# Dividing attention by its sums in packed feature lanes: four PE transposes a token block replaced by DMAs through DRAM

## The chip, the cores and the metric

The kernel runs on one core of a Trainium2 chip, as one launch. The metric is the device time of that launch in microseconds. Engines are named as the profile names them: PE (matrix), DVE (vector), ACT (scalar), POOL, and SP, whose queue issues most of the DMAs. The tile framework puts the waits between engines; within an engine instructions run in the order in which they stand, and a DMA's wait holds up everything behind it in its queue.

## What is computed

Two transformer layers over x of shape (8, 512, 256), float32, 16 heads of 16 features, a layer norm after each residual. Layer 0 is a masked softmax attention and a mixture of experts with a capacity of 512 tokens an expert. Layer 1 normalises q and k inputs by their mean square, rotates q and k, and takes sigmoid weights in place of exponentials; its mixture has eight experts and four that pass x through. What matters here:

```python
# layer 0: keys j at or behind query i
scores = einsum('bhid,bhjd->bhij', q, k) * 0.25
attn = softmax(where(j >= i, scores, -inf), -1)
out = einsum('bhij,bhjd->bhid', attn, v)
# layer 1
weights = sigmoid(einsum('bhqd,bhkd->bhqk', q, k) * 0.25)
weights = weights / (sum(weights, -1, keepdims=True) + 1e-8)
attn = einsum('bhqk,bhkd->bhqd', weights, v)
# both
x = layernorm(x + attn.reshape(8, 512, 256) @ o_w.T + o_b)
```

Both divide only after the weighted sum over v: the values carry a seventeenth column of ones for each head, so that the sum of the weights comes out beside the head's 16 features.

## The kernel before, in words

**Waves.** Each sequence's attention runs in 16 waves. A wave makes one block of scores for four heads (`scores`, L583 and L1021), ACT takes the exponential or sigmoid, and the wave after adds the weights times v into a PSUM bank (`gathered`, L607 and L1039). The four heads' lanes lie 32 apart: 16 features, one sum, 15 empty ones. After every fourth wave the bank is copied by ACT into `o`, a tile of 128 lanes by (t, m, token); t and m pick the head within its lane group. So o of sequence a is whole shortly after the next sequence b = a + 1 has begun its waves.

**From o to the projection.** In the waves of b, steps for a are placed by hand. `by_token` (L623, L1055; four a sequence) turns 128 tokens of o with four PE transposes into a bank of PSUM, where DVE takes the reciprocal of the 16 sums of a token and multiplies, into `ao` (token by feature). `by_feature` (L642, L1075; two a sequence) turns ao back with four transposes and a copy into `aoT` (feature by token). `projected` (L653, L1089) multiplies aoT by wo_s, four matmul groups a sequence, and adds the residual. The banks that these steps use (`bank`, tag mm) are one in layer 0 and two in layer 1.

**Order.** Within `tc.manual_schedule` the order on each engine is that of the program. `beside0(b, w)` and `beside1(b, w)` hold the plan of wave w: lists that run after the wave's scores (`first`), after the gather (`second`), and in layer 1 a third behind both. In layer 0 each wave also makes `greatest`, the search of row maxima six waves ahead, whose four reductions are DVE's largest work. Layer 1's plan also holds `query`, a part of q or k: after the second part ACT adds the bias (`raw`), POOL and DVE rotate it (L1009 to L1012), and for k DVE makes `kb` (L1017). `value`, `turned_in`, `normed` and `residual` prepare sequence n = b + 1.

**Other stages.** The steps of sequence 6 of layer 0 are laid into the gaps of that layer's expert matmuls (the list at L1624), those of sequence 7 into layer 1's first waves (L1540), and those of sequence 7 of layer 1 into the first blocks of its experts (L1831), each block of which is loaded by `load` (L1687), on SP, two blocks ahead.

**SP's queue** loads x, the weights and the blocks, and blanks DRAM buffers of layer 1 (`fill`, L472: per sequence 16 transfers of 272 KB and two of 512 KB, in four parts at waves 0, 4, 8 and 12). Layer 1's weights are issued where `layer1` is called, between waves 31 and 32 of layer 0 (L1607), and first read by PE in the first step of `router_steps` (`turn`, L277), in sequence 2's first wave. None of these waits for computed data until L1406 loads the tokens of the experts, so SP's place in the program says little of when it issues.

Of the kernel before, what the change touches and what calls it, by code (L numbers as in the profile page):

```python
# [9 lines left out]
FP = mybir.dt.float32  # L10
# [3 lines left out]
ALU = mybir.AluOpType  # L14
# [3 lines left out]
P = 128  # L18
# [5 lines left out]
NHS = 4  # L24
# [19 lines left out]
def tile_two_layers(  # L44
# [174 lines left out]
    def project(ps, w, hs, xT):  # L219
        for kc in range(KC):  # L220
            nc.tensor.matmul(
                out=ps, lhsT=w[:, kc, hs * P : (hs + 1) * P], rhs=xT[:, kc, :],
                start=(kc == 0), stop=(kc == KC - 1),
            )
# [136 lines left out]
    def layer0():  # L361
# [261 lines left out]
        def by_token(b, c):  # L623
            q = st[b]
            ps = bank()
            for t in range(2):
                for m in range(2):
                    nc.tensor.transpose(
                        ps[:, (2 * t + m) * P : (2 * t + m + 1) * P],
                        q["o"][:, t, m, c * P : (c + 1) * P], ident,  # L630
                    )
            ps = ps.rearrange("p (t h x) -> p t h x", t=2, x=32)
            rec = small.tile([P, 2, 8], FP, tag="rec", name="rec")
            nc.vector.reciprocal(rec, ps[:, :, :, HD])
            if c == 0:
                q["ao"] = att.tile([P, NC, D], FP, tag="ao", name=f"ao{b}")
            nc.vector.tensor_tensor(
                q["ao"][:, c, :].rearrange("p (h t x) -> p t h x", t=2, x=HD),
                ps[:, :, :, :HD], rec.unsqueeze(3).to_broadcast([P, 2, 8, HD]), ALU.mult,
            )  # L640

        def by_feature(b, kc):  # L642
            q = st[b]
            if kc == 0:
                q["aoT"] = att.tile([P, KC, S], FP, tag="aoT", name=f"aoT{b}")
            ps = bank()
            for c in range(NC):
                nc.tensor.transpose(
                    ps[:, c * P : (c + 1) * P], q["ao"][:, c, kc * P : (kc + 1) * P], ident
                )  # L650
            nc.scalar.copy(q["aoT"][:, kc, :], ps)
# [197 lines left out]
    def layer1(turns):  # L849
# [205 lines left out]
        def by_token(b, c):  # L1055
            q = st[b]
            ps = bank()
            for t in range(2):
                for m in range(2):
                    nc.tensor.transpose(  # L1060
                        ps[:, (2 * t + m) * P : (2 * t + m + 1) * P],
                        q["o"][:, t, m, c * P : (c + 1) * P], ident,
                    )
            ps = ps.rearrange("p (t h x) -> p t h x", t=2, x=32)
            rec = small.tile([P, 2, 8], FP, tag="rec", name="rec")
            nc.vector.tensor_scalar(rec, ps[:, :, :, HD], TINY, None, ALU.add)
            nc.vector.reciprocal(rec, rec)
            if c == 0:
                q["ao"] = att.tile([P, NC, D], FP, tag="ao", name=f"ao{b}")
            nc.vector.tensor_tensor(  # L1070
                q["ao"][:, c, :].rearrange("p (h t x) -> p t h x", t=2, x=HD),
                ps[:, :, :, :HD], rec.unsqueeze(3).to_broadcast([P, 2, 8, HD]), ALU.mult,
            )

        def by_feature(b, kc):  # L1075
            q = st[b]
            if kc == 0:
                q["aoT"] = att.tile([P, KC, S], FP, tag="aoT", name=f"aoT{b}")
            ps = bank()
            for c in range(NC):  # L1080
                nc.tensor.transpose(
                    ps[:, c * P : (c + 1) * P], q["ao"][:, c, kc * P : (kc + 1) * P], ident
                )
            if kc == 0:
                nc.vector.tensor_copy(q["aoT"][:, kc, :], ps)
            else:
                nc.scalar.copy(q["aoT"][:, kc, :], ps)
# [202 lines left out]
    def beside0(b, w):  # L1290
# [13 lines left out]
            1: ([(t.by_token, a, 0)], [(t.turned_in, n, 1), (t.pointed, z)]),  # L1304
            2: ([], [(t.query, n, 0, "q", 0), (t.residual, n), (t.kept, z, 0)]),
            3: ([(t.query, n, 0, "q", 1)], [(t.query, n, 0, "k", 0), (t.kept, z, 1)]),
            4: ([(t.by_token, a, 1)], [(t.by_token, a, 2), (t.counted, z)]),
            5: ([(t.by_token, a, 3)], [(t.ranked, z)]),
            6: ([], [(t.query, n, 0, "k", 1), (t.sent, z), (t.kept, z, 2)]),
            7: ([(t.by_feature, a, 0)], [(t.by_feature, a, 1), (t.kept, z, 3)]),  # L1310
# [44 lines left out]

    AHEAD = 6
    waiting = None

    def waves0(start, stop):
        nonlocal waiting  # L1360
        t = l0
        for g in range(start, stop):
            b, w = g // 16, g % 16
            now = None
            if g >= 0:
                now = t.scores(b, w // 8, w // 4 % 2, NC - 1 - w % 4)
                if w % 4 == 0:
                    t.fill(b, w // 4)
                if w == 10 and b + 2 < B:
                    t.load_x(b + 2)  # L1370
# [147 lines left out]
    def beside1(b, w):  # L1518
# [4 lines left out]
            0: ([], [(t.query, b, 1, "q", 1)], []),  # L1523
            1: ([(t.by_token, a, 0)], [(t.by_token, a, 1)], [(t.summed, n, 0), (t.scatter, z, 0)]),
            2: ([(t.by_token, a, 2)], [(t.by_token, a, 3)], [(t.summed, n, 1), (t.scatter, z, 1)]),
            3: ([], [(t.query, b, 1, "k", 0)], [(t.summed, n, 2), (t.scatter, z, 2)]),
            4: ([], [(t.query, b, 1, "k", 1)], []),
            5: ([(t.by_feature, a, 0)], [(t.by_feature, a, 1)], [(t.summed, n, 3), (t.scatter, z, 3)]),
            6: ([(t.projected, a, 0)], [], [(t.normed, n), (t.gather, f, 0)]),
            7: ([(t.projected, a, 1)], [(t.turned_in, n, 0)], [(t.residual, n), (t.gather, f, 1)]),  # L1530
            8: ([(t.projected, a, 2)], [(t.turned_in, n, 1)], [(t.gather, f, 2)]),
            9: ([(t.projected, a, 3)], [(t.query, n, 0, "q", 0)], [(t.normed3, a), (t.gather, f, 3)]),
            10: ([], [(t.query, n, 0, "q", 1)], [(t.logits, a)]),
            11: ([], [(t.query, n, 0, "k", 0)], [(t.chosen, a)]),
            12: ([], [(t.query, n, 0, "k", 1)], []),
            13: ([(t.value, n, 0)], [(t.value, n, 1)], [(t.counted, a)]),
            14: ([(t.value, n, 2)], [(t.ranked, a)], [(t.sent, a)]),
            15: ([(t.value, n, 3)], [(t.query, n, 1, "q", 0)], []),
        }
        if b == 0:  # L1540

            u, a = l0, B - 1
            for i, (first, second, third) in {
                0: ([(t.value, 0, 2)], [(t.query, 0, 1, "q", 0)], []),
                1: ([(t.value, 0, 3), (u.by_token, a, 0)], [(u.by_token, a, 1)], []),
                2: ([(u.by_token, a, 2)], [(u.by_token, a, 3)], []),
                5: ([(u.by_feature, a, 0)], [(u.by_feature, a, 1)], []),
# [52 lines left out]
    with tc.manual_schedule():  # L1600
# [20 lines left out]
        waiting = None  # L1621
        a, z, n = B - 2, B - 3, B - 1
        t = l0
        steps = [(t.by_token, a, 0), (t.query, n, 1, "q", 0), (t.by_token, a, 1), (t.query, n, 1, "q", 1)]  # L1624
        steps += [(t.by_token, a, 2), (t.query, n, 1, "k", 0), (t.by_token, a, 3), (t.query, n, 1, "k", 1)]
        steps += [(t.by_feature, a, kc) for kc in range(KC)]
        steps += [(t.kept, z, c) for c in range(NC)]
# [441 lines left out]
```

## Time and profile before

| | us |
|---|---|
| three runs, median (lowest to highest) | 1525.03 (1523.87 to 1526.2) |
| the profiled execution | 1510.96 |
| its span, first to last instruction | 1509.2 |

The mean granted PE clock of the profiled execution was 0.973. By stage, from the busy times of windows:

| stage | us | PE | DVE | ACT | POOL | DMA share |
|---|---|---|---|---|---|---|
| start and sequence 0 of layer 0 | 0 to 104 | 89.4 | 53.0 | 46.8 | 25.8 | 0.76 |
| layer 0's attention, sequences 1 to 6 | 104 to 520 | 390.6 | 283.2 | 215.4 | 134.2 | 0.32 |
| layer 0's experts | 520 to 735 | 212.3 | 48.1 | 34.2 | 0.0 | 0.24 |
| layer 0's last sequence, layer 1's first waves | 735 to 830 | 84.6 | 55.7 | 44.8 | 40.6 | 0.10 |
| layer 1's attention | 830 to 1273 | 429.2 | 311.7 | 288.2 | 180.7 | 0.16 |
| layer 1's expert blocks and the end | 1273 to 1509 | 201.1 | 127.8 | 61.8 | 99.0 | 0.64 |

A row of a group reads: line, engine, operation, tile written <- tiles read, shapes, count | busy us in all, mean ns of one | idle us of its engine just before, with the release that ended most of it. A row of a timeline reads: start, duration, engine, line, operation, count merged into the row [idle before <- what ended it]. One f32 matmul leaves two records, so a group of four matmuls is x8. A row of DMA issues gives the count, KB of each and the median us from issue to landing; SPq is SP's queue.

### The profile page before, as it was taken

What the parts mean: (1) busy time and instruction counts of PE and PEld (TensorE: products, weight loads), DVE (VectorE), ACT (ScalarE), POOL (GpSimd) and SP (SyncE); (2) the same over time, 40 slices, a digit from 0 to 9 for tenths busy, and PEclk for the clock granted to TensorE, in tenths of its full rate; (3) what the DMA queues carried; (4) which work ended last, traced back from release to release, by engine and by line L of the source; (5) the groups of instructions that cost most, each with busy time, mean ns of one, the idle gap of its engine ahead of it and who ended that gap; (6) DMA issues with size and microseconds to landing.
All of it is one profiled execution on the core that took longest, in us unless ns stands there. A gap on an engine that the chain in (4) does not pass through costs nothing. (4 is left out here: it accounts for less than half of the span.)

```text
span 1509.2 us, 24812 instructions
## 1 busy us (share of the span) xinstructions
PE 1407.2 (93%) x8574; PEld 762.1 (51%) x8574; DVE 879.6 (58%) x3287; ACT 691.2 (46%) x1079; POOL 480.3 (32%) x602
## 2 busy tenths in 40 slices
PE   7999989999998899999989999999999999999991
PEld 4444444444444466776534333334333334888881
DVE  4556666776767512321365766876876855553494
ACT  3455545555555321111235656666666665222242
POOL 2322233333233200000252224544653440442462
PEclk9999999999999999999979999999999999999996
DMA  9959960000000013223010000202302005677864
GB/s 243 265 149 355 358 229 17 14 13 19 7 23 4 30 49 119 84 84 98 29 42 6 24 9 30 41 27 24 46 26 25 20 20 168 185 219 214 281 218 157
DMA packets 136011, 149.86 MB, mean 99 GB/s; under 512 B 29646, under 2 KB 118891, under 8 KB 135875
## 3 DMA queue, kind: packets, MB, share of 16 engines
q1 hardware_dynamic: 118274, 121.51, 25.6%
q0 software_dynamic: 10560, 23.51, 6.1%
q10 hardware_dynamic: 7040, 3.15, 0.8%
q8 instruction: 72, 1.18, 0.3%
q14 instruction: 65, 0.52, 0.1%
HBM read 76.88 MB, written 77.10 MB: 102 GB/s over the span
## 5 line engine op out<-in xcount | busy, mean ns | idle before, releaser
L569 DVE CUSTOM_DVE_ANT_0 seen<-sc,shade 128x128 f32<-128x128 f32 (+3 forms) x512 | 250.9, 490 | 131.8 <-PE sc L561 102.4
L1035 ACT ACTIVATE e<-sc 128x1024 f32<-128x1024 f32 x256 | 248.3, 1021 | 148.9 <-PE sc L1027 147.4
L600 POOL TENSOR_SCALAR_AFFINE_SELECT e<-e 128x256 f32<-128x256 f32 x256 | 104.8, 414 | 576.9 <-ACT e L597 574.0
L597 ACT ACTIVATE e<-sc 128x1024 f32<-128x1024 f32 (+3 forms) x256 | 168.2, 702 | 129.8 <-PE sc L588 120.5
L588 PE MATMUL sc<-q,k 32*128 32x512 f32 (+3 forms) x1024 | 140.6, 500 | 7.6 <-DVE mpad L569 7.0
L1044 PE MATMUL av<-e,v 128*32 128x512 f32 x1024 | 139.6, 612 | 0.0
L561 PE MATMUL sc<-k,q 32*128 32x384 f32 (+3 forms) x1024 | 120.8, 489 | 5.8 <-DVE mpad L569 4.6
L612 PE MATMUL av<-e,v 128*32 128x512 f32 (+3 forms) x1024 | 101.2, 464 | 2.7 <-POOL e L600 2.3
L1457 PE MATMUL sc<-wo,h 128*128 128x256 f32 x448 | 99.2, 380 | 0.0
L1748 PE MATMUL yp<-w_e,h 128*128 128x256 f32 x416 | 96.2, 384 | 2.2 <-DVE h L1740 2.2
L1440 PE MATMUL sc<-xeT,wi 128*128 128x512 f32 x224 | 98.3, 592 | 0.0
L1732 PE MATMUL sc<-xtT,w_e 128*128 128x256 f32 x416 | 94.2, 379 | 0.0
L588 PEld LDWEIGHTS sc<-q,k 32*128 32x128 f32 x1024 | 57.9, 190 | 66.7 <-issue 36.7
L1457 PEld LDWEIGHTS sc<-wo,h 128*128 128x128 f32 x448 | 84.3, 190 | 11.5 <-issue 0.5
L1748 PEld LDWEIGHTS yp<-w_e,h 128*128 128x128 f32 x416 | 79.8, 193 | 13.7 <-DVE h L1740 2.6
L1759 POOL DMA_INDIRECT ybuf<-yt,to x52 | 51.0, 981 | 111.0 <-DVE yt L1758 101.2
L1732 PEld LDWEIGHTS sc<-xtT,w_e 128*128 128x128 f32 x416 | 77.2, 190 | 9.5
L1027 PE MATMUL sc<-q,k 16*128 16x512 f32 x512 | 77.4, 644 | 4.2 <-PEq L1654 2.6
L1027 PE MATMUL sc<-q,kb 32*128 32x512 f32 x512 | 77.3, 640 | 0.4 <-ACT e L1035 0.4
L1210 POOL DMA_INDIRECT xbuf<-x,idx x64 | 68.0, 1062 | 23.8 <-issue 15.3
L561 PEld LDWEIGHTS sc<-k,q 32*128 32x128 f32 x1024 | 51.2, 186 | 47.0 <-issue 24.2
L898 POOL DMA_INDIRECT got<-ybuf,idx_all x64 | 65.5, 1024 | 17.3 <-issue 14.3
(304 smaller groups left out, 2087.4 us busy)
## 6 DMA issues: line engine op xcount, KB each, us to landing
xbuf<-blank SPq DMA_DIRECT2D x130, 272.0 KB, 6.8
w_e<-in_w SPq DMA_DIRECT2D x104, 256.0 KB, 3.5
ybuf<-blank SPq DMA_DIRECT2D x16, 512.0 KB, 6.9
y<-ybuf SPq DMA_DIRECT2D x16, 512.0 KB, 5.7
wi<-in_we_in SPq DMA_DIRECT2D x7, 1024.0 KB, 6.7
wo<-in_we_out SPq DMA_DIRECT2D x7, 1024.0 KB, 9.1
xt<-xbuf SPq DMA_DIRECT2D x26, 272.0 KB, 3.5
own<-in_x SPq DMA_DIRECT2D x8, 512.0 KB, 6.6
```

The lines of the kernel that those rows point to most:

```text
L561: nc.tensor.matmul(out=places[r], lhsT=q["q", m, t][32 * r : 32 * r + 32, ib * P : (ib + 1) * P], rhs=q["k", m, t][32 * r : 32 * r + 32, i ...
L569: nc.vector.tensor_tensor_reduce(out=seen[:, :width], in0=places[r], in1=shade[:, :width], scale=-1.0, scalar=-MASKED, op0=ALU.add, op1=AL ...
L588: nc.tensor.matmul(out=places[r], lhsT=q["k", m, t][32 * r : 32 * r + 32, jb * P : (jb + 1) * P], rhs=q["q", m, t][32 * r : 32 * r + 32, : ...
L597: nc.scalar.activation(e[:, :, :width], s[:, :, :width], AF.Exp, scale=SCALE)
L600: nc.gpsimd.affine_select(out=own, in_=own, pattern=[[0, 2], [-1, P]], compare_op=ALU.is_ge, fill=0.0, base=0, channel_multiplier=1,)
L612: nc.tensor.matmul(out=q["av"][32 * r : 32 * r + 32, : (jb + 1) * P], lhsT=vs[b % 2][:, jb, 8 * m + 2 * r + t, :], rhs=es[r], start=(jb == ...
L1027: nc.tensor.matmul(out=scs[r // 2][:, r % 2, :], lhsT=k[32 * r : 32 * r + lanes, jb * P : (jb + 1) * P], rhs=q["q", m][32 * r : 32 * r + l ...
L1035: nc.scalar.activation(e, scs[pr], AF.Sigmoid, scale=SCALE)
L1044: nc.tensor.matmul(out=q["av"][32 * r : 32 * r + 32, :], lhsT=vs[b % 2][:, jb, 8 * m + 2 * r + t, :], rhs=es[r // 2][:, r % 2, :], start=( ...
L1457: nc.tensor.matmul(out=ps[:, c, :], lhsT=h[f][:, c * P : (c + 1) * P], rhs=wo[:, f, :], start=(f == 0), stop=(f == I0 // P - 1),)
L1732: nc.tensor.matmul(out=ps[:, f // 2, f % 2 * TB : (f % 2 + 1) * TB], lhsT=q.wi[kc][:, f * P : (f + 1) * P], rhs=q.xtT[:, kc, :], start=(kc ...
L1748: nc.tensor.matmul(out=q.ps[c], lhsT=q.h[:, f // 2, at : at + P], rhs=q.wo[f // 2][:, f % 2 * D : (f % 2 + 1) * D], start=(f == 0), stop=( ...
```

## The change

The transposes to tokens and back go. Three steps take their place. `moved` (as `apart_again`) sends o's sum lanes to DRAM in one DMA (4 lanes of 2048), loads them as 128 lanes of 64, and brings o's values with eight DMAs (16 lanes of 1024 each, SBUF to SBUF) to the packed feature lanes of `ao`. `shares` (as `inverted`) takes the reciprocal of the 128 by 64 sums on DVE, stores it to DRAM and loads it into `aoT`, each of its eight rows of 1024 read for 16 lanes. `divided` (as `weighed`) multiplies aoT by ao on DVE, 128 by 512 twice. All twelve DMAs of a sequence are on SP. `projected` is as before.

In layer 0's plan the three stand at waves 1, 4 and 7, and `fill` moves to waves 6, 8, 10 and 12. In layer 1's they stand at waves 1, 3 and 5, in the third list; values 2 and 3 and the queries of m = 1 move to waves 0 to 5, one a wave, and turned_in to waves 8 and 9. The lists for the experts' gaps and for the last blocks are changed likewise. An unused function, `project`, is removed.

```diff
+    def moved(q, b):
+        o = q["o"]
+        nc.sync.dma_start(
+            out=sums_d[b % 2].rearrange("(g j) i -> g (j i)", g=NHS),
+            in_=o[HD::32].rearrange("p t m n -> p (t m n)"),
+        )
+        q["sums"] = small.tile([P, NH * S // P], FP, tag="sums_c", name="sums_c")
+        nc.sync.dma_start(out=q["sums"], in_=sums_d[b % 2])
+        q["ao"] = att.tile([P, KC, S], FP, tag="ao", name=f"ao{b}")
+        for t in range(2):
+            for g in range(NHS):
+                at = 32 * g + HD * t
+                nc.sync.dma_start(out=q["ao"][at : at + HD], in_=o[32 * g : 32 * g + HD, t])
+
+    def shares(q, b, least):
+        if least:
+            nc.vector.tensor_scalar(q["sums"], q["sums"], least, None, ALU.add)
+        nc.vector.reciprocal(q["sums"], q["sums"])
+        nc.sync.dma_start(out=shares_d[b % 2], in_=q["sums"])
+        q["aoT"] = att.tile([P, KC, S], FP, tag="aoT", name=f"aoT{b}")
+        rows = shares_d[b % 2].rearrange("(h j) i -> h (j i)", h=2 * NHS)
+        nc.sync.dma_start(
+            out=q["aoT"], in_=rows.unsqueeze(1).to_broadcast([2 * NHS, HD, KC * S])
+        )
+
+    def divided(q, kc):
+        t = q["aoT"][:, kc, :]
+        nc.vector.tensor_tensor(t, t, q["ao"][:, kc, :], ALU.mult)
...
-            1: ([(t.by_token, a, 0)], [(t.turned_in, n, 1), (t.pointed, z)]),
+            1: ([], [(t.turned_in, n, 1), (t.pointed, z), (t.apart_again, a)]),
...
-            4: ([(t.by_token, a, 1)], [(t.by_token, a, 2), (t.counted, z)]),
-            5: ([(t.by_token, a, 3)], [(t.ranked, z)]),
+            4: ([], [(t.counted, z), (t.inverted, a)]),
+            5: ([], [(t.ranked, z)]),
...
-            7: ([(t.by_feature, a, 0)], [(t.by_feature, a, 1), (t.kept, z, 3)]),
+            7: ([], [(t.weighed, a, 0), (t.weighed, a, 1), (t.kept, z, 3)]),
...
+    FILLS = (6, 8, 10, 12)
...
-                if w % 4 == 0:
-                    t.fill(b, w // 4)
+                if w in FILLS:
+                    t.fill(b, FILLS.index(w))
...
-            0: ([], [(t.query, b, 1, "q", 1)], []),
-            1: ([(t.by_token, a, 0)], [(t.by_token, a, 1)], [(t.summed, n, 0), (t.scatter, z, 0)]),
-            2: ([(t.by_token, a, 2)], [(t.by_token, a, 3)], [(t.summed, n, 1), (t.scatter, z, 1)]),
-            3: ([], [(t.query, b, 1, "k", 0)], [(t.summed, n, 2), (t.scatter, z, 2)]),
-            4: ([], [(t.query, b, 1, "k", 1)], []),
-            5: ([(t.by_feature, a, 0)], [(t.by_feature, a, 1)], [(t.summed, n, 3), (t.scatter, z, 3)]),
+            0: ([], [(t.value, b, 2)], []),
+            1: ([], [(t.value, b, 3)], [(t.apart_again, a), (t.summed, n, 0), (t.scatter, z, 0)]),
+            2: ([], [(t.query, b, 1, "q", 0)], [(t.summed, n, 1), (t.scatter, z, 1)]),
+            3: ([], [(t.query, b, 1, "q", 1)], [(t.inverted, a), (t.summed, n, 2), (t.scatter, z, 2)]),
+            4: ([], [(t.query, b, 1, "k", 0)], [(t.summed, n, 3), (t.scatter, z, 3)]),
+            5: ([], [(t.query, b, 1, "k", 1)], [(t.weighed, a, 0), (t.weighed, a, 1), (t.gather, f, 0)]),
             6: ([(t.projected, a, 0)], [], [(t.normed, n), (t.gather, f, 1)]),
...
-        steps += [(t.by_token, b, c) for c in range(NC)]
+        steps += [(t.apart_again, b)]
         steps += [(t.scatter, b - 1, c) for c in range(NC)]
-        steps += [(t.by_feature, b, kc) for kc in range(KC)]
-        steps += [[]]
+        steps += [(t.inverted, b)]
+        steps += [[]] * 3
+        steps += [(t.weighed, b, kc) for kc in range(KC)]
         steps += [(t.projected, b, c) for c in range(NC)]
```

More of the change, by code (lines that the diff above doesn't have):

```diff
@@ L217, in transposed @@
         return t
[L219 to L224, printed above, removed]
+    sums_d = [dram.tile([P, NH * S // P], FP, name=f"sums_d{i}") for i in range(2)]
+    shares_d = [dram.tile([P, NH * S // P], FP, name=f"shares_d{i}") for i in range(2)]
+    def moved(q, b):
[24 more added lines that the diff above has]
+        nc.vector.tensor_tensor(t, t, q["ao"][:, kc, :], ALU.mult)
     def rsqrt(v, shape, tag):
@@ L620, in gathered, with apart_again, inverted, weighed @@
                 nc.scalar.copy(q["o"][:, t, m, :], q["av"])
[L623 to L651, printed above, removed]
+        def apart_again(b):
+            moved(st[b], b)
+        def inverted(b):
+            shares(st[b], b, None)
+        def weighed(b, kc):
+            divided(st[b], kc)
         def projected(b, c):
@@ L1052, in gathered, with apart_again, inverted, weighed @@
                 nc.scalar.copy(q["o"][:, t, m, :], q["av"])
[L1055 to L1087, printed above, removed]
+        def apart_again(b):
+            moved(st[b], b)
+        def inverted(b):
+            shares(st[b], b, TINY)
+        def weighed(b, kc):
+            divided(st[b], kc)
         def projected(b, c):
@@ L1529, in beside1 @@
[L1529 to L1538, printed above, removed]
+            0: ([], [(t.value, b, 2)], []),
+            1: ([], [(t.value, b, 3)], [(t.apart_again, a), (t.summed, n, 0), (t.scatter, z, 0)]),
+            2: ([], [(t.query, b, 1, "q", 0)], [(t.summed, n, 1), (t.scatter, z, 1)]),
@@ new lines, in beside1 @@
+            3: ([], [(t.query, b, 1, "q", 1)], [(t.inverted, a), (t.summed, n, 2), (t.scatter, z, 2)]),
+            4: ([], [(t.query, b, 1, "k", 0)], [(t.summed, n, 3), (t.scatter, z, 3)]),
+            5: ([], [(t.query, b, 1, "k", 1)], [(t.weighed, a, 0), (t.weighed, a, 1), (t.gather, f, 0)]),
+            6: ([(t.projected, a, 0)], [], [(t.normed, n), (t.gather, f, 1)]),
+            7: ([(t.projected, a, 1)], [], [(t.residual, n), (t.gather, f, 2)]),
+            8: ([(t.projected, a, 2)], [(t.turned_in, n, 0)], [(t.gather, f, 3)]),
@@ L1539, in beside1 @@
+            9: ([(t.projected, a, 3)], [(t.turned_in, n, 1)], [(t.normed3, a)]),
+            10: ([], [(t.query, n, 0, "q", 0)], [(t.logits, a)]),
+            11: ([], [(t.query, n, 0, "q", 1)], [(t.chosen, a)]),
+            12: ([], [(t.query, n, 0, "k", 0)], []),
+            13: ([], [(t.query, n, 0, "k", 1)], [(t.counted, a)]),
+            14: ([(t.value, n, 0)], [(t.ranked, a)], [(t.sent, a)]),
+            15: ([], [(t.value, n, 1)], []),
         }
@@ L1543, in beside1 @@
             for i, (first, second, third) in {
[L1544 to L1547, printed above, removed]
+                1: ([], [], [(u.apart_again, a)]),
+                3: ([], [], [(u.inverted, a)]),
+                5: ([], [], [(u.weighed, a, 0), (u.weighed, a, 1)]),
                 6: ([(u.projected, a, 0)], [], []),
@@ L1623, in tile_two_layers @@
         t = l0
-        steps = [(t.by_token, a, 0), (t.query, n, 1, "q", 0), (t.by_token, a, 1), (t.query, n, 1, "q", 1)]
-        steps += [(t.by_token, a, 2), (t.query, n, 1, "k", 0), (t.by_token, a, 3), (t.query, n, 1, "k", 1)]
-        steps += [(t.by_feature, a, kc) for kc in range(KC)]
+        steps = [(t.apart_again, a)]
+        steps += [(t.query, n, 1, which, part) for which in "qk" for part in range(2)]
+        steps += [(t.inverted, a)]
         steps += [(t.kept, z, c) for c in range(NC)]
+        steps += [(t.weighed, a, kc) for kc in range(KC)]
         steps += [(t.projected, a, c) for c in range(NC)]
```

## The prediction

> **What bounds the kernel now.** I read the page's busy times first, then the groups of instructions by line, then the timelines of PE, DVE and SP through one period of each stage, since only those show what an instruction's removal frees.
>
> ```profile
> PE 1407.2 (93%) x8574; PEld 762.1 (51%) x8574; DVE 879.6 (58%) x3287; ACT 691.2 (46%) x1079; POOL 480.3 (32%) x602
> L1060 PE MATMUL mm<-ident,o 128*128 128x128 f32 x128 | 20.6, 284 | 2.9 <-DVE rec L1066 2.0 <-ACT xtT L1717 0.8
> L628 PE MATMUL mm<-ident,o 128*128 128x128 f32 x128 | 20.5, 283 | 3.5 <-DVE turns L279 0.8 <-DVE lgx L987 0.6 <-DVE gsum L301 0.5
> L648 PE MATMUL mm<-ident,ao 128*128 128x128 f32 x64 | 10.4, 285 | 0.6
> L1081 PE MATMUL mm<-ident,ao 128*128 128x128 f32 x64 | 10.4, 285 | 0.0
> ```
>
> PE is the bound, and the transposes that go make 384 records (62 us busy). Records overlap: in the timeline a group of four starts 0.58 to 0.59 us before its successor among the 512-wide attention matmuls, 0.44 us among the expert matmuls. So a sequence's six groups are 3.5 us there and 2.6 us here. Whether that comes back depends on what ends next in each stage.
>
> **Layer 1's attention** (eight sequences, period 58.3 us from the first transpose at 1110.05 to the next sequence's at 1168.36). PE's rows and then DVE's:
>
> ```profile
> 1179.42 1.13 PE L999 MATMUL mm<-xnT,wk_s 128*128 128x256 f32 x4
> 1180.49 1.14 PE L1027 MATMUL sc<-q,kb 32*128 32x512 f32 x8
> 1185.46 1.17 PE L1093 MATMUL mm<-wo_s,aoT 128*128 128x268 f32 x4 [0.59 <-DVE aoT L1085]
> 1191.48 1.21 PE L964 MATMUL mm<-ident,xn 128*128 128x128 f32 x4 [0.69 <-DVE xn L938]
> ...
> 1181.55 0.74 DVE L1010 STREAM_SHUFFLE turned<-raw 128x512 f32<-128x512 f32 x1
> 1184.72 0.68 DVE L1085 COPY aoT<-mm 128x512 f32<-128x512 f32 x1
> ```
>
> PE has hardly a gap: the bracketed 0.59 and 0.69 and a 0.34 us wait on the reciprocal's bank are the 1.6 us it idles. All three go (no transposed banks; turned_in moves a wave behind normed), and so do 3.5 us of transposes: 58.3 - 3.5 - 1.6 = 53.2 us of PE.
> What is late next is the product. In wave 5 DVE's order is the k chain (shuffle, two products, kb), then weighed; PE's first work after scores(6) is projected, which reads both products. From the rows: the k query leaves PE at 1180.49 and the chain ends at 1184.72, 4.2 us later. Two products of 128x512 at 694 ns (the row of L1012) end 5.6 us after it. PE needs the first after 1.1 us of scores and the second 0.55 us later, so it **stalls 4.0 us** even if all data are there.
> The shares come later still. Take wave 4's start as 0. The q chain of wave 3 ends at 3.4 (ACT 0.1 + 0.7, DVE 2.6), and the reciprocal stands behind it on DVE: add 0.2, reciprocal of 64 columns some 0.45 (252 ns for 16 columns, 182 for 4, extended), done at 4.05. SP then writes the shares (2.0 us, the landing of 32 KB for cos_s), waits for them (0.25 with semaphores) and loads them 16-fold, 512 KB. No row has this transfer. Near rows:
>
> ```profile
> wi<-in_we_in SPq DMA_DIRECT2D x7, 1024.0 KB, 6.7
> ybuf<-ye SPq DMA_DIRECT2D x7, 512.0 KB, 3.2
> ```
>
> By size alone the row says 3.2 us, a store of as many bytes. The Trainium skill (DMA: Bandwidth & Descriptors, "Why a DMA increments its semaphore by 16 and not by 1") speaks against the change: a DMA uses the largest number of engines, at most 16, that divides the slowest dimension of both sides. The source's is 8 (eight rows, each repeated), so 8 engines carry 64 KB each, which is what each of 16 carries for the 1 MB row at 6.7 us. I take 5.2, between them, nearer the second because it too reads DRAM. With 5.2 the shares land at 11.55, the products end at 12.3 and 13.0, and projected ends at 13.55. Unstalled (two waves of 3.2, scores 1.1, projection 1.1) it would end at 8.6. **Stall 5.0 us**: period 58.2, or no change (0 x 8). At 3.2 the k chain decides (4.0 us): -1.1 each, -9 in all. At 6.7 the stall is 6.5: +1.5 each, +12. Within the stall nothing else proceeds on PE; behind weighed on DVE stand projected's sums and normed, which PE next needs only two waves later (some 6 us of DVE work against 6.4), so no second stall.
> The early half is covered: o is copied half a wave into wave 1, the sums make two trips (about 4.6 us) and eight loads of ao at 0.45 to 0.63 us of issue on SP end about 9 us in, while the reciprocal comes at 13.
>
> **Layer 0's attention** (six sequences, period 68.1 us, of which PE's own work at unstalled durations is some 61: 36 in three attention matmuls a wave, 17 in the projections, 8 in transposes and ranks). Here transposes sit inside waits:
>
> ```profile
> 331.11 0.65 PE L628 MATMUL mm<-ident,o 128*128 128x128 f32 x4
> 331.70 1.01 PE L561 MATMUL sc<-k,q 32*128 32x128 f32 x8
> ...
> 345.97 1.97 PE L588 MATMUL sc<-q,k 32*128 32x512 f32 x8
> 347.88 1.16 PE L657 MATMUL mm<-wo_s,aoT 128*128 128x264 f32 x4
> ...
> 347.64 0.69 DVE L569 CUSTOM_DVE_ANT_0 seen<-sc,shade 128x512 f32<-128x512 f32 x1
> ```
>
> The L561 of 128 columns takes 1.01 where it needs 0.43: it waits for ACT to leave a score bank. The group ahead of it, and likewise wave 1's, was hidden: 0. The two of wave 4's end and wave 5 give 0.7 to 0.8 (the rank matmul's bank, behind DVE, keeps the rest); by_feature's first group with its 0.17 us bank wait brings the lead to about 1.1 at the 512-wide search of wave 7. Then weighed follows that search's four reductions on DVE, which end at 348.3 now and at 347.2 then; products at 347.9 and 348.5, projected ends at 349.15 against 348.96. So **+0.2 us** a sequence, +1.2. Bounds: -0.7 if DVE runs ahead, +1.0 if POOL's concurrent work stretches the products as it stretches L1011 (1221 ns): -4 to +6. The shares themselves have three waves (12 us) for their 8 us. ACT loses two copies of 0.59 and DVE about 1 us net a sequence; neither ends a wait there.
>
> **Experts of layer 0** (the last-but-one sequence's steps): PE is gapless at 520 to 735 us. Six groups, five at 0.44, and the bank waits 1.51 and 0.24 behind the first and before the last transposes of o: **-4.2 us**. SP reaches the steps' DMAs before the next weights. Five gaps and a second projection block cover the shares.
> **Tail** (layer 1's last sequence beside the expert blocks): **-2.6 us**, six groups at 0.43. SP now holds the loads of blocks 3 and 4 behind o's last copy and behind the reciprocal; both still land about when their transposes want them. If not, +3.
>
> **SP's order.** This is what the short description doesn't tell. Now SP runs ahead of everything:
>
> ```profile
> 57.51 4.06 SPq L489 DMA_DIRECT2D xbuf<-blank  x4
> 61.62 4.81 SPq L262 DMA_DIRECT2D wq_s<-in_wq  x2
> 93.28 5.03 SPq L254 DMA_DIRECT2D wo_s<-in_wo  x8
> ...
> 169.68 0.44 PE L277 MATMUL mm<-ident,wo_s 128*128 128x128 f32 x2
> ```
>
> Layer 1's weights are issued by 98 us and first read by PE at 169.7. In the changed order SP, before it issues them, must wait for sequence 0's o and for its reciprocal in wave 4 of sequence 1. That is at 124 us (331.11 stands 212 us behind the same place, and DVE gets there at 336). Shares out and in take 2.8, sequence 1's fills some 12 (19 transfers, 8 of them left in flight), then 36.7 us as in the rows (61.6 to 98.3) and 2 to land: 177 to 181. PE waits at the first turning of wo_s: **+9 us once**, 5 to 12. The cover that held it was 70 us of slack. Spreading the other fills over layer 0 costs nothing: they follow the shares and are read in layer 1.
>
> **Sum**: 0 + 1.2 - 4.2 - 2.6 + 9 = +3.4 us. Against the profiled execution (1510.96, span 1509.2) that is 1514; the runs' median stands 14 us higher, so **1528.5 us**. A difference under 0.2% (3 us) can't be told from none.
>
> **The rivals.**
> A, faster: the shares land by the k chain (3.2 us) and layer 1's weights are only 5 us late, with layer 0 at -0.3 a sequence: -9 - 2 - 4.2 - 2.6 + 5 = -13, 1512. For it: nine tenths of PE busy, and an idle DMA in layer 1 (its share is 0.16). Against it: the two-trip chain and the order on DVE. 22 in 100. The full 62 us would need every wait above to vanish: 2 in 100.
> B, much slower: the aoT load in layer 1 at 6.7 us and the store at 2.7 give a stall of 7.2 a sequence, +2.2 x 8 = 17; with the weights' 9, layer 0 at +0.5 a sequence (3) and the gains of 6.8, +22: 1547. Place: DVE's wait for aoT before weighed in wave 5. It decides once store and load pass 6.3 us together (below that the k chain does), and each us beyond costs 8. For it: the rule of engines. 24 in 100.
> C, no change, near-cancelling: within the forecast's spread. Forecast itself (1518 to 1536): 52.
>
> The forecast's 52 split into 3 faster, 18 same and 31 slower, since its middle lies just past the edge of what can be told. With A and the full gain: faster 0.27; same 0.18; with B: slower 0.55. The range takes in most of A and B: 1512 to 1546.
>
> **What would show it.** Layer 1's period near 58, with PE idle about 5 us before projected in each, released by DVE's product, and DVE waiting for the aoT DMA; the landing of that DMA near 5; one PE wait of about 9 us on wo_s near 170; layer 0's period still near 68; no transpose of o or ao. Wrong if the period of layer 1 falls to 54, if wo_s arrives in time, or if the load of aoT takes far more or less than 5 us.

## The result, and the profile after

The changed kernel took 1572.01 us (median of 4 runs, 1566.48 to 1577.68) against 1524.45 before (4 runs, 1518.87 to 1526.2): a ratio of 1.0319, 95% interval 1.0272 to 1.0365. It is slower by some 48 us where the forecast was 3.4. The profiled executions are 1573.32 (span 1571.5) and 1510.96 (span 1509.2), 62.3 us apart in span; what follows accounts for those 62.3. The profiled execution of before is 8 to 15 us under its four timed runs and as fast as its runs beside the experiments (about 1510), so the change may cost nearer 60 than 48; why the four were longer is not known.

The page of the changed kernel first: its busy times, its busy tenths of PE, and the row of the clock that PE was granted.

```profile
PE 1389.0 (88%) x8190; PEld 738.0 (47%) x8190; DVE 850.4 (54%) x3175; ACT 680.0 (43%) x1055; POOL 482.2 (31%) x602
PE   7999699999998899999888988989789889799991
PEclk9999879999997999999968899999899999899996
```

The 384 records are gone, but PE is busy only 18.2 us less, not 62. The last row tells most of why: PE's matmuls ran longer. Before, the same row was almost whole (a 9 is 90% or more):

```profile
PEclk9999999999999999999979999999999999999996
```

The mean granted clock fell from 0.973 to 0.937. So I split each stage's time three ways: PE idle (no matmul record running), half-clock loss (half of the time that PE was busy under a granted clock of 0.5), and the rest, PE's work at full clock (so the loss is an estimate: it takes what ran at half clock to need twice its time). Stages end where a sequence's last copy into o starts.

| stage | before | after | difference | PE idle | half-clock loss | work |
|---|---|---|---|---|---|---|
| start, sequence 0 of layer 0 | 104.6 | 106.0 | +1.3 | +0.5 | 0.0 | +0.8 |
| layer 0, sequences 1 and 2 | 143.7 | 156.8 | +13.1 | +11.9 | +7.3 | -6.0 |
| layer 0, sequences 3 to 5 | 204.4 | 202.9 | -1.5 | +7.1 | 0.0 | -8.5 |
| layer 0, sequence 6 | 68.0 | 73.3 | +5.3 | +1.3 | +8.4 | -4.5 |
| experts of layer 0, its last sequence | 282.6 | 283.0 | +0.4 | +0.6 | +2.1 | -2.3 |
| layer 1's eight sequences | 470.1 | 504.5 | +34.4 | +48.4 | +17.4 | -31.4 |
| tail | 235.7 | 244.9 | +9.2 | +10.7 | +0.3 | -1.8 |
| sum | 1509.2 | 1571.5 | +62.3 | +80.5 | +35.5 | -53.7 |

**Layer 1.** Over half of it is here. The costliest group of its projection waits for DVE's product nearly all of its idle time:

```profile
L1077 PE MATMUL mm<-wo_s,aoT 128*128 128x268 f32 x128 | 44.0, 473 | 45.4 <-DVE aoT L254 45.1
```

One stall (the third sequence), in PE's timeline, then DVE's and SP's rows that lead up to it:

```profile
1038.88 1.19 PE L1036 MATMUL sc<-q,kb 32*128 32x512 f32 x8
1046.21 2.15 PE L1077 MATMUL mm<-wo_s,aoT 128*128 128x268 f32 x4 [6.14 <-DVE aoT L254]
1048.30 1.52 PE L1053 MATMUL av<-e,v 128*32 128x512 f32 x8
1049.75 1.14 PE L1036 MATMUL sc<-q,kb 32*128 32x512 f32 x8
```

```profile
1036.27 0.55 DVE L244 RECIPROCAL sums_c<-sums_c 128x64 f32<-128x64 f32 x1
...
1043.47 0.69 DVE L1021 TENSOR_TENSOR k<-k,turned 128x512 f32<-128x512 f32 x1 [2.06 <-POOL k L1018]
1044.20 0.49 DVE L1026 TENSOR_SCALAR kb<-k,odd 128x512 f32<-128x512 f32 x1
1045.41 1.35 DVE L254 TENSOR_TENSOR aoT<-aoT,ao 128x512 f32<-128x512 f32 x2 [0.72 <-DMA aoT<-shares_d]
```

```profile
1036.85 0.33 SPq L245 DMA_DIRECT2D shares_d<-sums_c  x1
1038.30 0.65 SPq L248 DMA_DIRECT2D aoT<-shares_d  x1
```

PE stands 6.14 us, as forecast in place and cause (5.0 was forecast). The load of aoT is issued at 1038.30 and lands at 1045.3: 7.0 us (6.4 to 7.3 in the eight stalls). The k chain (L1019 to L1026) ends just ahead of it, at 1044.7, because POOL's part of it is late by 2 us. Then look at the lengths behind the stall: the projection takes 2.15 where its next one takes 1.17, the gather 1.52 where it takes 1.06. The windows of the same stretch (start and end, length, busy time of PE with its count, of the weight loads, DVE, ACT and POOL; then granted clock, DMA share, GB/s) show the clock:

```profile
1040.00:1042.00 2.00, 0.07 (x4) 0.00 (x0) 1.38 (x2) 1.96 (x4) 1.93 (x2) 1.00 0.57 181
1042.00:1044.00 2.00, 0.00 (x0) 0.00 (x0) 0.53 (x1) 0.45 (x2) 1.83 (x3) 0.61 0.49 118
1044.00:1046.00 2.00, 0.00 (x0) 0.00 (x0) 1.24 (x3) 0.00 (x0) 1.70 (x2) 0.50 0.18 49
1046.00:1048.00 2.00, 1.79 (x4) 1.17 (x4) 0.76 (x2) 0.00 (x0) 1.47 (x2) 0.50 0.52 90
1048.00:1050.00 2.00, 2.00 (x13) 0.46 (x16) 1.46 (x8) 0.00 (x0) 1.01 (x1) 0.68 0.61 74
```

In the trace's record of the clock it halves 2.4 us into the stall and is whole again 3 us after it. So each stall is paid a second time: here about 1.4 us, 1.0 on the projection and 0.5 on the gather. There are eight such stalls, 5.61 to 8.17 us long, 51.8 us in all.

**Layer 0 and the tail.** PE's wait for layer 1's weights came where it was forecast, 9.98 us for 9:

```profile
181.09 0.66 PE L307 MATMUL mm<-ident,wo_s 128*128 128x128 f32 x2 [9.98 <-DMA wo_s<-in_wo]
```

In the tail SP, which also loads the expert blocks, stands in the waits of the last sequence's DMAs (SP's rows, then PE's):

```profile
1340.20 0.42 SPq L245 DMA_DIRECT2D shares_d<-sums_c  x1
1346.27 0.72 SPq L248 DMA_DIRECT2D aoT<-shares_d  x1
1348.93 0.39 SPq L1676 DMA_DIRECT2D xt<-xbuf  x1
```

```profile
1340.09 0.63 PE L1698 MATMUL mm<-ident,xt 128*128 128x128 f32 x4 [2.15 <-DMA xt<-xbuf]
1355.85 1.09 PE L1698 MATMUL mm<-ident,xt 128*128 128x128 f32 x4 [8.22 <-DMA xt<-xbuf]
```

SP waits 5.6 us between the store of the shares and their load: the store, issued right behind 1 MB of expert weights, lands after 6.1 us where it took 1.4 in most sequences. So the tokens of a block are issued only at 1348.93. They then land after 6.8 us, beside the 512 KB load of aoT, where before's took 2.8 to 4.7; PE waits 8.22 us for them.

### The profile page after: what moved, and what is told of

Same layout as the page of the kernel before. It is cut to its first block, busy times and chain, and to the rows that moved or that the text cites. A ratio compares the mean times of both kernels' runs of the same rounds, so it can differ in the third digit from the quotient of the medians.

```text
span 1571.5 us, 24275 instructions
## 1 busy us (share of the span) xinstructions
PE 1389.0 (88%) x8190; PEld 738.0 (47%) x8190; DVE 850.4 (54%) x3175; ACT 680.0 (43%) x1055; POOL 482.2 (31%) x602
## 5 line engine op out<-in xcount | busy, mean ns | idle before, releaser
L591 PE MATMUL sc<-k,q 32*128 32x384 f32 (+3 forms) x1024 | 132.2, 502 | 13.2 <-DVE mpad L599 6.6
L1053 PE MATMUL av<-e,v 128*32 128x512 f32 x1024 | 143.6, 633 | 0.0
L1442 PEld LDWEIGHTS sc<-wo,h 128*128 128x128 f32 x448 | 85.9, 193 | 12.3 <-issue 0.5
L591 PEld LDWEIGHTS sc<-k,q 32*128 32x128 f32 x1024 | 55.6, 195 | 68.1 <-issue 24.1
L1733 PEld LDWEIGHTS yp<-w_e,h 128*128 128x128 f32 x416 | 78.7, 190 | 13.4 <-DVE h L1725 2.9
L1077 PE MATMUL mm<-wo_s,aoT 128*128 128x268 f32 x128 | 44.0, 473 | 45.4 <-DVE aoT L254 45.1
```

The lines of the kernel that those rows point to most:

```text
L591: nc.tensor.matmul(out=places[r], lhsT=q["q", m, t][32 * r : 32 * r + 32, ib * P : (ib + 1) * P], rhs=q["k", m, t][32 * r : 32 * r + 32, i ...
L1053: nc.tensor.matmul(out=q["av"][32 * r : 32 * r + 32, :], lhsT=vs[b % 2][:, jb, 8 * m + 2 * r + t, :], rhs=es[r // 2][:, r % 2, :], start=( ...
L1442: nc.tensor.matmul(out=ps[:, c, :], lhsT=h[f][:, c * P : (c + 1) * P], rhs=wo[:, f, :], start=(f == 0), stop=(f == I0 // P - 1),)
L1733: nc.tensor.matmul(out=q.ps[c], lhsT=q.h[:, f // 2, at : at + P], rhs=q.wo[f // 2][:, f % 2 * D : (f % 2 + 1) * D], start=(f == 0), stop=( ...
```

## The experiments

Theory: three waits made by order (the product in layer 1, the weights, the blocks' tokens) and a clock that follows PE's waits. Rivals: the clock drops for another reason; and the wait in layer 1 is too much work on DVE, whatever its order. Beside these runs before took about 1510 us (five medians of 7 runs, 1509.6 to 1510.3; single runs 1507 to 1519), and kernels whose edit had next to no effect on the time took 1567 to 1575.

**What the idle stretch itself costs.** Matmuls of constants fill the stall.

```diff
+        def busied(n):
+            ps = bank()
+            for _ in range(n):
+                nc.tensor.matmul(out=ps, lhsT=ident, rhs=cos_s, start=True, stop=True)
...
+            if w == 6:
+                l1.busied(9)
```

> Nine matmuls of constants (128x512, 0.59 us each, 5.3 us) are put on PE between the scores of wave 6 and projected in layer 1, where PE stands idle 5.6 to 8.2 us; their result is read by nothing. Theory (the idle stretch itself makes the granted clock drop, and the drop costs 1.4 us a sequence after the stall): projected still starts when DVE's product is there, but the half-clock stretches at these eight places go, the first projection takes 1.17 us instead of 2.15, the period goes from 61.6 to about 60.2, the whole from 1572 to about 1560. Rival (the drops have another cause: the DMAs or the matmuls around them): half-clock stretches stay, period 61.6, 1572.

1566.06 us, ratio 1.0374 (1.0343 to 1.0406). The half-clock stretches at these stalls all went, but nine matmuls took 7.99 us, longer than the stall, so the period stayed 61.7. The fill was mis-sized; six were tried next.

> As e1_fill_stall with six matmuls in place of nine: nine took 7.7 us (0.86 each), more than the stall they were to fill; six take 5.2, within it. Theory (the idle stretch makes the clock drop): projected starts when it did, no half-clock stretch at these places, layer 1's period 61.6 - 1.5 = 60.1, the whole about 12 us under the changed kernel's 1572. Rival (the drop costs nothing by itself, or has another cause): period 61.6.

1557.25 us, ratio 1.0306 (1.0268 to 1.0343); PE at one stall:

```profile
1034.87 5.42 PE L1076 MATMUL mm<-cos_s,ident 128*128 128x512 f32 x12
1040.72 1.27 PE L1082 MATMUL mm<-wo_s,aoT 128*128 128x268 f32 x4 [0.43 <-DVE aoT L254]
1041.92 1.06 PE L1053 MATMUL av<-e,v 128*32 128x512 f32 x8
```

The projection still waits for the product, but runs at full speed behind the fill. The period is 60.0 in three sequences and 61.2 to 61.5 in two; half-clock loss in sequences 2 to 7 fell from 10.4 to 1.7 us. Work that nothing reads made the kernel 10 to 18 us faster than those whose edit had no effect: the idle stretch brings the clock down, and the DMAs and matmuls around it, which stayed, do not.

**Which of two chains holds the product.**

```diff
-            2: ([], [(t.query, b, 1, "q", 0)], [(t.summed, n, 1), (t.scatter, z, 1)]),
-            3: ([], [(t.query, b, 1, "q", 1)], [(t.inverted, a), (t.summed, n, 2), (t.scatter, z, 2)]),
+            2: ([], [(t.query, b, 1, "q", 0)], [(t.inverted, a), (t.summed, n, 1), (t.scatter, z, 1)]),
+            3: ([], [(t.query, b, 1, "q", 1)], [(t.summed, n, 2), (t.scatter, z, 2)]),
```

> Only inverted moves, from wave 3 to wave 2, ahead of the q chain on DVE. Theory (the shares' two DMAs end last before the product, the k chain just before them): DVE's waits for the load of aoT go (0.2 to 2.8 us in layer 1, 3.1 in the first waves, 12 us over the eight), the product starts as soon as kb is done, the stall shrinks from 6.5 to about 5 us, the whole to about 1560; the clock still drops at each stall. Rival (the k chain alone decides): no change, 1572.

1567.45 us, ratio 1.0371 (1.0347 to 1.0394). DVE's wait for aoT went, the product starts right behind kb, and the stalls are 3.55 to 5.63 (mean 4.9 for 6.5). One of them (PE):

```profile
1048.03 2.15 PE L1077 MATMUL mm<-wo_s,aoT 128*128 128x268 f32 x4 [5.30 <-DVE aoT L254]
```

So the k chain alone holds PE for 5.2 to 5.6 us in the last six of the eight. But the time hardly moved: the clock came back later relative to the stall's end, and half-clock loss in sequences 2 to 7 rose from between 1.5 and 2.1 us a period to between 2.1 and 2.6. A stall that is only shortened keeps its second price.

```diff
-            5: ([], [(t.query, b, 1, "k", 1)], [(t.weighed, a, 0), (t.weighed, a, 1), (t.gather, f, 0)]),
+            5: ([], [(t.weighed, a, 0), (t.weighed, a, 1), (t.query, b, 1, "k", 1)], [(t.gather, f, 0)]),
```

> Only weighed moves, ahead of the k query in wave 5, so that on DVE the product stands before the k chain. Theory (the shares' DMAs end last): the product starts at the same place, stall and period unchanged (6 us, 61.6), the k chain is done 2 us later, which nothing awaits before wave 8: 1572, give or take 4. Rival (the k chain decides): the stall falls to about 1.5 us, the clock stays full, 1572 - 8 x 6 = 1524.

1569.43 us, ratio 1.0412 (1.0372 to 1.0452): no change, stalls 5.4 to 6.5 (mean 5.9). DVE now waits 5.0 to 7.9 us for the DMA. So the shares' DMAs alone hold PE nearly as long as both chains do: the theory of two chains of nearly equal length stands.

**Both out of the way.** The two edits together, and projected a wave later.

```diff
-            6: ([(t.projected, a, 0)], [], [(t.normed, n), (t.gather, f, 1)]),
-            7: ([(t.projected, a, 1)], [], [(t.residual, n), (t.gather, f, 2)]),
+            6: ([], [], [(t.normed, n), (t.gather, f, 1)]),
+            7: ([(t.projected, a, 0)], [], [(t.residual, n), (t.gather, f, 2)]),
...
+            10: ([(t.projected, a, 3)], [(t.query, n, 0, "q", 0)], [(t.normed3, a)]),
```

> Three moves in layer 1's plan together: inverted in wave 2, weighed ahead of the k query in wave 5, the four parts of projected one wave later (7 to 10, with normed3 and logits after them). Theory (each of the two chains alone would hold the product, together they are moved out of PE's way, and the clock follows the stall): the eight stalls (51.8 us in all) and the half-clock stretches behind them (13 us) go, layer 1's period falls from 61.6 to 53 to 54 us, the whole to about 1507. Rival (the load of aoT takes so long that even a wave and a half more does not cover it): the stall stays above 2 us, the period above 56, the whole above 1525.

1542.44 us, ratio 1.0224 (1.0175 to 1.0274): the stall at projected is gone (0.5 us is left), so the rival's cause is ruled out, but the time is the rival's: another stall appears two waves on (PE):

```profile
1035.58 1.06 PE L1053 MATMUL av<-e,v 128*32 128x512 f32 x8
1038.72 0.72 PE L973 MATMUL mm<-ident,xn 128*128 128x128 f32 x4 [2.08 <-DVE lgx L1084]
1039.38 2.09 PE L1036 MATMUL sc<-q,k 16*128 16x512 f32 x8
```

DVE has summed, the product, the k chain and normed in one row; PE waits 2.08 us for the end of that row (xn, and lgx right behind it). That is enough for the clock: the scores behind it take 2.09 for 1.14, and four periods are 61.3 to 61.6, where one without half clock is 56.9. The next kernel takes work out of that row and loads out of SP's (`some(q, i, j)` issues loads i to j of ao).

```diff
+            0: ([], [(t.value, b, 2)], [(t.summed, n, 0), (t.summed, n, 1)]),
+            1: ([], [(t.value, b, 3)], [(t.apart_again, a), (t.summed, n, 2), (t.summed, n, 3), (t.scatter, z, 0)]),
...
+        some(q, 0, 3)
         nc.sync.dma_start(out=q["sums"], in_=sums_d[b % 2])
...
         nc.sync.dma_start(out=shares_d[b % 2], in_=q["sums"])
+        some(q, 3, 6)
```

> The moves of e4_no_stall, and two more: summed in waves 0 and 1 (e4 showed the next wait: DVE, with summed, the product, the k chain and normed in one row, was 2 us late with xn, and the clock dropped again), and on SP the eight loads of ao are spread into the two places where SP waits for a landing, three, three and two, so that the shares' DMAs need not stand behind all eight. Theory: no PE gap above 1.2 us in layer 1's periods, no half-clock stretch there, period 53 to 54, the whole 1503 to 1512. Rival (DVE has too much work in these waves whatever its order): a gap of 2 us or more stays in each period, the clock drops, period 57 to 61, the whole above 1530.

1547.43 us, ratio 1.0231 (1.0188 to 1.0275): the rival's numbers. Its cause is not shown, for the order was wrong: the four parts of summed stood ahead of the reciprocal, and the last two loads of ao stood behind the 512 KB of aoT. DVE's row of the product (L259 in that kernel):

```profile
1035.25 3.21 DVE L259 TENSOR_TENSOR aoT<-aoT,ao 128x512 f32<-128x512 f32 x2 [5.02 <-DMA ao<-o]
```

**SP's order.** Layer 1's loads are issued 16 waves earlier.

```diff
-        waves0(-AHEAD, 32)
+        waves0(-AHEAD, 16)
...
-        waves0(32, 48)
+        waves0(16, 48)
```

> Only the loads of layer 1's weights are issued 16 waves earlier, before sequence 1's moved on SP. Theory (SP's order holds them): the wait of 9.98 us on wo_s near 181 us goes, and the half-clock stretch behind it (10.2 us, of which some 5 are lost); sequences 1 and 2 together 157 us become 142 to 147: the whole 10 to 15 us under 1572. Rival (the loads are late because the fills share the DMA engines with them): the wait stays above 5 us.

1554.14 us, ratio 1.03 (1.0249 to 1.0351). The wait is gone (PE):

```profile
170.59 0.44 PE L307 MATMUL mm<-ident,wo_s 128*128 128x128 f32 x2
```

Sequences 1 and 2 take 141.2 us for 156.8, and the whole is 18 us under 1572, more than the 10 to 15 expected. The same transfers are made, so it was the order.

In the tail, the twelve DMAs of the last sequence go to another queue (`moved` and `shares` take it as an argument).

```diff
-            moved(st[b], b)
+            moved(st[b], b, nc.gpsimd if b == B - 1 else nc.sync)
...
-            shares(st[b], b, TINY)
+            shares(st[b], b, TINY, nc.gpsimd if b == B - 1 else nc.sync)
```

> Only the twelve DMAs of layer 1's last sequence go to POOL's queue. Theory (SP stands in these DMAs' waits, and the blocks' tokens and weights behind it come late): PE's waits on xt of 2.15 and 8.22 us go, the tail takes 245 - 10 - 2 = 233 us (before: 235.7), the whole about 12 us under 1572. Rival (the loads are late by traffic or buffers, or POOL's own work now holds the shares): the wait on xt or on the product stays above 4 us.

1575.2 us, ratio 1.0412 (1.037 to 1.0454): the rival. The waits on xt went, so SP's order had made them; but on POOL the shares stand behind its own scatters (their reciprocal is done at 1340.3), come later still, and the first projection waits (POOL's rows, then PE's):

```profile
1353.58 0.60 POOL L245 DMA_DIRECT2D shares_d<-sums_c  x1
1356.50 0.66 POOL L248 DMA_DIRECT2D aoT<-shares_d  x1 [2.32 <-issue]
1364.42 1.89 PE L1077 MATMUL mm<-wo_s,aoT 128*128 128x268 f32 x3 [14.82 <-DVE gx L1704]
```

The row names gx, which DVE makes just behind the first half of the product (1363.63 to 1364.32); DVE itself had stood idle for 17 us ahead of that.

**All together.** The plan of waves 2 and 4, layer 0's product, and the tail's transposes:

```diff
+            2: ([], [(t.query, b, 1, "q", 0)], [(t.inverted, a), (t.summed, n, 2), (t.summed, n, 3), (t.scatter, z, 1)]),
+            4: ([], [(t.query, b, 1, "k", 0)], [(t.weighed, a, 0), (t.weighed, a, 1), (t.normed, n), (t.scatter, z, 3)]),
...
-            7: ([], [(t.weighed, a, 0), (t.weighed, a, 1), (t.kept, z, 3)]),
+            7: ([(t.weighed, a, 0), (t.weighed, a, 1)], [(t.kept, z, 3)]),
...
-        steps += [(t.apart_again, b)]
+        steps += [(t.by_token, b, c) for c in range(NC)]
```

> All parts together. Layer 1: inverted in wave 2 ahead of summed 2 and 3, summed 0 and 1 in wave 0, weighed and normed in wave 4 ahead of the k query, projected in waves 7 to 10, and on SP all loads of ao ahead of that of aoT (e6 showed the product waiting 5 us for the last two of ao, behind the 512 KB). Layer 0: weighed ahead of the search of wave 7. Layer 1's weights issued before wave 16. The last sequence of layer 1 again by transposes. Theory (each loss is a wait that an order makes, and the clock follows a wait of 2 us): layer 1's period 53 to 55 with no half-clock stretch, layer 0's sequences 1 and 2 together 140 to 147, layer 0's period 66.5, the tail 235: 1475 to 1490, under before (about 1510 on this chip) by some 25. Rival (the sums and the values in DVE's row of work around wave 5 are too much in any order): a gap of 2 us stays in layer 1, period 58 to 61, the whole 1515 to 1535.

1540.01 us, ratio 1.0189 (1.0169 to 1.0209). That is 50 us over the theory and above the rival too. The weights and the tail (235.8) came as expected, layer 1 did not: with normed ahead of the k chain, k is 3.1 to 3.8 us late. And layer 0 got worse by 4.4 us in each of three sequences, because the product, now ahead of the search of maxima, waits for its DMA and makes the search late (PE):

```profile
285.35 2.08 PE L623 MATMUL sc<-q,k 32*128 32x512 f32 x4 [3.65 <-DVE mpad L604]
```

Two corrections follow: layer 0's product back in its place, and normed split, its root into DVE's wait for aoT.

```diff
-            4: ([], [(t.query, b, 1, "k", 0)], [(t.weighed, a, 0), (t.weighed, a, 1), (t.normed, n), (t.scatter, z, 3)]),
-            5: ([], [(t.query, b, 1, "k", 1)], [(t.gather, f, 0)]),
-            6: ([], [], [(t.gather, f, 1)]),
+            4: ([], [(t.query, b, 1, "k", 0)], [(t.mean_rooted, n), (t.scatter, z, 3)]),
+            5: ([], [(t.weighed, a, 0), (t.weighed, a, 1), (t.query, b, 1, "k", 1)], [(t.gather, f, 0)]),
+            6: ([], [], [(t.mean_scaled, n), (t.gather, f, 1)]),
```

> e9_all_ordered with two corrections. Layer 0's weighed goes back behind the search of wave 7 (e9 showed DVE waiting 2.5 us there for the load of aoT, mpad late by 3.7 us, and the clock half: 4 us a sequence lost). Layer 1: the small operations of normed (its root) alone stand in wave 4, where DVE waits 2 to 3 us for the load of aoT; then the product, the k chain, and xn in wave 6. Theory: no PE gap above 1.2 us in layer 1's periods, no half clock in them, period 53 to 55; layer 0's sequences 3 to 5 at 67.6 again: e9's 1540 - 13 - 5 x 6 = 1490 to 1500, under before (1510). Rival (as in e4, e6 and e9, the wait only moves to the next reader on DVE): a gap of 2 us in each period, 58 to 61, the whole above 1520.

1490.98 us (1489.81 to 1491.57), ratio 0.9877 (0.9861 to 0.9894): 1.2% faster than before, as the theory had it. PE through the place of the stall:

```profile
1002.79 1.06 PE L1066 MATMUL av<-e,v 128*32 128x512 f32 x8
1003.99 2.04 PE L1049 MATMUL sc<-q,kb 32*128 32x512 f32 x8
1005.96 1.17 PE L1124 MATMUL mm<-wo_s,aoT 128*128 128x268 f32 x4
1007.06 1.06 PE L1066 MATMUL av<-e,v 128*32 128x512 f32 x8
```

The projection (L1124 in this kernel) starts without a wait behind the scores of waves 6 and 7, which share a row. Layer 1's period is 54.9 us in five sequences (61.5 to 64.2 in the changed kernel, 58.3 before), with 1.2 us idle and no half clock. The same twelve DMAs a sequence are there; only order differs (the last sequence is by transposes). Whether before would gain from a new order too was not run; PE idles only 1.6 us a period there, without half clock, so that could give at most half of the 3.4 us.

In layer 0 the projections are then moved behind the gather.

```diff
-            8: ([(t.projected, a, 0)], [(t.projected, a, 1)]),
-            9: ([(t.projected, a, 2)], [(t.projected, a, 3)]),
-            10: ([], [(t.query, n, 1, "q", 0)]),
+            8: ([], [(t.projected, a, 0)]),
+            9: ([(t.projected, a, 1)], [(t.projected, a, 2)]),
+            10: ([(t.projected, a, 3)], [(t.query, n, 1, "q", 0)]),
```

> e10_root_in_the_wait, and in layer 0 the four parts of projected stand half a wave to a wave later (8 second, 9, 9, 10 first), behind the gather. Theory (the 1.05 us wait of each sequence's first projection then lies beside the gather): layer 0's period 67.6 - 1 = 66.6, five sequences 5 us, and fewer windows under two thirds busy, so half-clock stretches in sequences 2 and 6 shrink: 5 to 15 us under e10. Rival (the single bank of layer 0 hands the wait on to the query behind the projections): no change, within 3 us of e10.

1492.49 us, ratio 0.9886 (0.9869 to 0.9902): the rival. The wait of 1.05 us went from five of the six first projections, but one of 0.8 us for DVE's q (L616) came at the fourth; layer 0's period, where no half clock fell, stayed 67.6, and half-clock loss in sequences 1 to 6 was 18.7 us for 15.2.

The last one puts transposes of the identity back where layer 0 had those of o.

```diff
-            4: ([], [(t.counted, z), (t.inverted, a)]),
-            5: ([], [(t.ranked, z)]),
+            4: ([(t.busied, a)], [(t.busied, a), (t.counted, z), (t.inverted, a)]),
+            5: ([(t.busied, a)], [(t.ranked, z)]),
```

> e10_root_in_the_wait, and in layer 0 four groups of four transposes of the identity a sequence, read by nothing, at the places in waves 1, 4, 4 and 5 where before had its transposes of o, which lay under PE's waits for ACT and DVE. Theory (work that fills waits holds the granted clock up): layer 0's half-clock loss, 15 us in e10's sequences 1 to 6 (12 to 23 in the runs without these transposes, 3.4 in before), falls to 3 to 6; the groups themselves cost up to 0.7 us a sequence where no wait covers them: 5 to 10 us under e10's 1491. Rival (the loss is a matter of where the windows of 3.41 us fall): the loss stays above 12, and the time is 0 to 4 us over e10.

1495.58 us, ratio 0.9902 (0.9864 to 0.9939). Layer 0's half-clock loss in sequences 1 to 6 is 7.8 us for 15.2, less than half but not the 3 to 6 expected, and the time did not fall (4.6 us over e10, nearest to the rival). Without such fills the loss was 8.4 (e7) to 28 (e9), so one trace proves little. Whether layer 0's loss comes from the missing transposes or from where the clock's windows fall stays open.

## Why the prediction was wrong

| term | forecast | measured | what |
|---|---|---|---|
| layer 1, eight sequences | 0 | +34.4 | eight stalls of 6.5 for 5.0, 11.8; a new wait of 1.0 in seven, 7.1; clock 17.4; the rest -1.9 |
| start, sequence 0 | 0 | +1.3 | |
| layer 1's weights late | +9 | +12.3 | wait 10.0, right in place and size; clock 2.3 behind it |
| layer 0, sequences 1 and 2 otherwise | +0.4 | +0.8 | clock 5.0, the rest -4.2 |
| layer 0, sequences 3 to 5 | +0.6 | -1.5 | the product's wait of 1.05 came, the hidden groups gave a little more |
| layer 0, sequence 6 | +0.2 | +5.3 | clock 8.4 |
| experts of layer 0 | -4.2 | -0.3 | PE works 2.0 less; idle time as before (waits of 0.37 to 1.24 in place of those of 1.51 and 0.24), clock 1.7 |
| layer 0's last sequence | 0 | +0.7 | |
| tail | -2.6 | +9.2 | waits on xt 2.15 and 8.22 |

The places were read rightly: where PE would stand in layer 1 and at the weights, and on what. The step that failed was "**Stall 5.0 us**: period 58.2, or no change (0 x 8)". It was to cost nothing and cost 34.4 us. It fails in three ways.

First, it charges a stall its own length. Nothing in the sum has a term for the granted clock, which made 35.5 of the 62.3 us; even rival B, with a stall of 7.2, lacks it. It could have been seen: before's own clock record has a half-clock stretch right behind the 2.59 us gap that ends at 869.07, and one behind the 2.48 us gap at 195.46, and a stall of 5 us was forecast eight times over. The Trainium skill (TensorE: Matmul & The Clock Gate, Part 1) says that an idle window of about 3.4 us puts the PE clock to half and a busy one of that length brings it back; by that rule alone a stall of 5 us takes in a whole such window in about half of the cases ((5.0 - 3.4) / 3.4), and then loses half of the 3.4 to 6.8 us up to the end of a whole busy window: some 1.2 us a stall, 1528.5 + 8 x 1.2 = 1538 (an estimate from the skill's figure). The traces show more: every one of the eight stalls was followed by half clock.

Second, the size of the load of aoT: "I take 5.2, between them" where it took 7.0 (6.4 to 7.3 in the eight stalls). The row of 1 MB at 6.7 and the rule of eight engines had said it, and the trace agrees with that rule: the load leaves one semaphore event 1.07 us after its issue and eight more, the last at 7.0, where the 32 KB store leaves sixteen. This is rival B's mechanism, and its stall of 7.2 is nearer to the 6.5 than mine. The store's term hid part of the error: 2.25 us were forecast for it and its wait, and 1.5 passed from the reciprocal's end to the issue of the load. (The reciprocal itself took 0.55 for the 0.45 of the forecast; its two figures, extended, give 0.53.) e3 measures these DMAs alone: stalls of 5.9 us in the mean where the forecast had 5.0.

Third, the k chain, 4.2 forecast and 5.8 measured: the change moves the last scatter from wave 5 to wave 4 and the k query's second part from wave 4 to wave 5, so that POOL's product of k now stands behind two indirect DMAs and a scaling, until 1042.19. I counted DVE's queue at the new place and not POOL's. e2 measures this chain alone: stalls of 5.2 to 5.6 us in six sequences where the forecast had 4.0. Beside the load of 7.0 it added little: with this chain out of the way (e3) the stalls were 5.9 us in the mean for 6.5.

The gain of the 1.6 us of bank waits was half right: they went, and a wait of 1.02 us on took (L1144) came.

In the tail "both still land about when their transposes want them" failed: each DMA of the twelve that waits for a landing makes SP wait too, 5.6 us once the landing shares the engines with weights. I gave that +3; PE's two waits on xt were worth 10.4.

That slower came out, at 55 in 100, was in part luck: of the sum's terms only the weights (+9) pulled that way and came true, and of the gains set against them in the experts and the tail 0.3 us came. Of the 35.5 us of half clock, 13.4 in layer 0 (5.0 in sequence 2, 8.4 in sequence 6) do not lie right behind one of these stalls; their cause stays open.

## What to carry to other kernels

In a kernel like this one, price a PE stall of 2 us or more at its length and some 1.5 to 3.4 us behind it, for each time it comes; shortening it gained little here until it was under 2 us. When a chain of DMAs takes the place of PE work, write down for every engine and queue it passes (POOL and SP too) what stands ahead of it and behind it, and start it so early that the longest landing seen for as many engines, not for as many bytes, is covered. The change was sound but for the last sequence, and its order was not: the same DMAs reordered, with that sequence left to transposes, gave 1491 us for 1510.

## What the runs showed of the hardware

In all fourteen traces the granted clock changes only at steps of 3.41 us. I counted, for each step at full clock behind another such step (the last 30 us of each trace left out), PE's busy share in it and whether the next step was at half. Under 40% busy: 92 of 92. 40 to 60%: 45 of 61. 60 to 70%: 57 of 188. 70 to 85%: 33 of 443. Over that: 2 of 4541. So it takes no idle step: of those under 60% busy 137 of 153 were followed by half clock, of those from 60 to 70% three in ten. The gaps of 2.07 to 2.13 us in e4 and e6, with gaps of some 0.5 us near them, were followed by half clock in 7 of 7 cases, the two of 1.88 us in one. These gaps are shorter than the 3.4 us of idleness that the Trainium skill speaks of (the page and part named above). In layer 0's sequences 3 to 6, where (e9 apart) no wait of PE is longer than 1.6 us, steps fall under that share now and then, and losses of 0 to 8.5 us a sequence come and go between kernels that are alike there.
